# Moving twelve pairs of one batch's feed-forward part from beside the last projections to beside the last causal convolution

## The chip, the cores and the metric

The kernel runs on one core of one Trainium2 chip. The metric is the time of one execution on the device, in microseconds (us). A core has five engines, each with a queue of its own: TensorE (PE in the profile) for matmuls, VectorE (DVE), ScalarE (ACT), GpSimd (POOL) and SyncE (SP), which here only issues transfers. GpSimd issues transfers too. All data are 32-bit floats.

## The reference

Two layers are computed on `x` of shape 4 x 512 x 128 x 64 (4 batches, 512 times, 8192 channels in all). Layer 0, cut to what matters here:

```python
xn = layernorm(x, ln_attn)                    # over the 8192 channels
k, v, r = xn @ Wk, xn @ Wv, sigmoid(xn @ Wr)  # 64 states each
states = scan(s = decay * s + k * v)          # over time
x = x + (r * states) @ Wo
x = x + gelu(conv_freq(layernorm(x, ln_freq)))        # 3 taps over the 128 frequencies
to = conv_time(layernorm(x, ln_time)) + time_b        # causal, 3 taps over time, per channel
x = x + layernorm(to, time_ln)
x = x + gelu(x @ ffn_W1 + b1) @ ffn_W2 + b2           # per group of 64 channels: 64 -> 256 -> 64
```

Layer 1 takes a moving average over time, filters the rest in the frequency domain, and adds both. The change does not touch it.

## The kernel before

**Tiling.** In layer 0 the 8192 channels of a batch are 64 chunks (`NCH`) of 128 partitions with the 512 times along the free dimension; two chunks are a pair (`NPR` = 32), and a transfer moves a pair (512 KB). Between stages a batch lies in DRAM: `x2d` after attention and frequency convolution, `tod` for the outcome of the causal convolution, `x4` after the feed-forward part.

**Stages of a batch.** `project` (J) multiplies the input with the key, value and gate weights; each step is one chunk, with loads of `xp`, of the weights `wx` and of the same input in time order for the statistics, which VectorE takes (L338), and it scales the weights (L355). `scan` (Z) is a long chain over several engines. `attend_and_convolve` (A) adds attention and does the frequency convolution. `convolve_time` (C) normalizes each pair (`normed`, L608 and L611), applies three taps (`tapped`: ScalarE L616, VectorE L620, four half-size operations a pair), squares the outcome, and has TensorE sum both for the next layer norm (`add_up`, L251). `open_feed` (O) spreads the moments of that norm into two rows of 512 times on all partitions (`rows`), and prepares two pairs. `feed_forward` (F) does the rest.

**Inside the feed-forward part.** `residual` loads `kx` (from `x2d`) and `kh` (from `tod`) and normalizes with two full-size VectorE operations (L686, L687). `add_residual` scales on ScalarE (L695) and adds on VectorE (L698). Per chunk, `widen` (L718) makes two products with the first weights into the tiles `m` and `c`, each followed by a GELU on ScalarE (L722) into `mid`; `narrow` (L729) multiplies with the second weights into `pa`, a PSUM tile of which there is one, and VectorE adds bias and residual while it evicts it (L734); `store` (L743) transposes on TensorE, ScalarE copies into `ob`, and GpSimd sends a transfer for every two pairs.

**Order.** TensorE's instructions stand in the order in which the program writes them (`manual_schedule`); a scheduler orders the other engines' queues, except where `keep_in_program_order` pins one. `in_turn` writes two lanes side by side: each line of its table holds two stages (or groups of stages) of different batches, each stage yields weights that add up to its share, and the lane that is behind goes on, with a lead that a list gives for each line. `needed` holds a stage back until its input exists. The lines around the change are:

```python
((1, (O, 0.05), (F, 0.95)), (3, (J, 0.88), (Z, 0.12))),
((2, (C, 1.0)), (3, (A, 1.0))),
((2, (O, 0.05), (F, 0.95)), (3, (C, 0.95), (O, 0.05))),
((3, (F, 1.0)), (3, (nothing, 1.0))),
```

So batch 1's feed-forward part goes beside batch 3's projections and scan, batch 2's beside batch 3's causal convolution, and batch 3's alone. While the feed-forward parts of batches 0 and 1 run, `convolve_ahead` makes the first 14 pairs (`AHEAD`) of the next batch's causal convolution, one step (`normed` or `tapped`) with every second chunk from the fifth on.

**Rows.** The spread rows live in single buffers by name: `rm`, `rm3` and `rm4`. A stage whose rows use a name waits until the last reader of the former rows is done.

Of the kernel before, what the change touches and what calls it, by code (L numbers as in the profile page):

```python
# [16 lines left out]
P = 128  # L17
# [4 lines left out]
NCH = D // P  # L22
SL = 512
NS = D // SL
NPR = NCH // 2
# [54 lines left out]
def layer0(ctx, tc, dram, x, xt, vecs, wkvr, wo, wdec, wconv, fbias, w1, fb1, w2, fb2, x4):  # L80
# [560 lines left out]
    def convolve_time(b):  # L641
        bank = of_a if b == B - 1 else of_p
        made = AHEAD if b in ahead else 0
        moment = carried.pop(b)
        if made:
            rb, mb = ahead.pop(b)
        else:
            rb, mb = yield from rows(bank, *moment, "rm" if b == B - 1 else "rm3")
        st = bank()
        waiting, added = [], 0  # L650
        n = NPR - made
        for k in range(n + 2):
            while waiting and waiting[0][0] == k - 2:
                add_up(st, 0, *waiting.pop(0)[1:], added == 0, added == NPR - 1)
                added += 1
            if k < n:
                if b == B - 1:

                    x2, xr, to, sq = spare("xp", SL), spare("x1", SL), spare("z", SL), two(bk, "sq")
                else:  # L660
                    x2 = bk.tile([P, 2, SL], F32, tag="kx", name="x2", bufs=3)
                    xr, to = two(bk, "kd"), bk.tile([P, 2, SL], F32, tag="k3", name="to", bufs=3)
                    sq = bk.tile([P, 2, SL], F32, tag="sq4", name="sq4", bufs=2)

                normed(b, made + k, x2, xr, rb, mb, made > 0 and k < 4)
                tapped(b, made + k, xr, to)
                nc.scalar.activation(sq, to, AF.Square)
                waiting.append((k, to, sq))
                i = k * made // n
                if i != (k + 1) * made // n:  # L670

                    to = fetch("kh", tod, b, i)
                    sq = bk.tile([P, 2, SL], F32, tag="mid", name="sq5", bufs=4)
                    nc.scalar.activation(sq, to, AF.Square)
                    waiting.append((k, to, sq))
            yield 7.0 * (NPR + 2) / (n + 2)
        mean, sq = yield from finish(st, bank, 4)
        causal[b] = moments(mean, sq, 4)

# [20 lines left out]

    def open_feed(b):
        last = b == B - 1
        scale[b] = yield from rows(of_a if last else of_p, *causal.pop(b), "rm3" if last else "rm4")
        opened[b] = {}
        for i in range(2):
            opened[b][i] = add_residual(b, i, *residual(b, i))
            yield CHAIN

    def feed_forward(b):
        x3s = opened.pop(b)  # L710
        mids, x4s, obs = {}, {}, {}

        def widen(c, m):
# [24 lines left out]
        def store(c):  # L738
# [2 lines left out]
            pt = pool.tile([P, NT, P], F32, tag=tag, name="pt")  # L741
            for t in range(NT):
                nc.tensor.transpose(pt[:, t, :], x4t[:, t * P : (t + 1) * P], ident)  # L743
            s = c // 4
            if c % 4 == 0:
                obs[s] = bk.tile([P, NT, SL], F32, tag="ob", name="ob")
            o = obs[s][:, :, c % 4 * P : (c % 4 + 1) * P]
            if c // 2 % 2:
                for h in range(2):
                    nc.scalar.copy(o[:, :, halves[1 - h]], pt[:, :, halves[h]])  # L750
            else:
                nc.scalar.copy(o, pt)
            if c % 4 == 3:
                nc.gpsimd.dma_start(
                    x4[b][:, s * SL : (s + 1) * SL].rearrange("(t p) d -> p t d", p=P), obs.pop(s)
                )

        early = None
        for c in range(NCH + 2):
            if c < NCH:  # L760
                widen(c, 0)
                widen(c, 1)
            i = c // 2 + 2
            if i < NPR:
                if c % 2:
                    x3s[i] = add_residual(b, i, *coming)
                else:
                    coming = residual(b, i)
            if 0 < c <= NCH:
                narrow(c - 1)  # L770
            if c > 1:
                store(c - 2)
            if b + 2 < B and c > 4 and c % 2:
                early = early or convolve_ahead(b + 1)
                next(early, None)
            yield 4.5

# [6 lines left out]
    def run(b, stages):  # L784
        for stage, share in stages:
            for weight in stage(b):
                yield BLOCKED if weight == BLOCKED else weight * share / whole[stage]

    def in_turn(leads, *pairs):
        at, running = [0.0, 0.0], [None, None]  # L790
# [26 lines left out]
    def nothing(b):  # L817
        yield 1.0

    J, Z, A, C, O, F = project, scan, attend_and_convolve, convolve_time, open_feed, feed_forward  # L820
    begin[A] = 0
    needed = {A: scanned, C: carried, O: causal, F: opened}
    whole = {
        J: 2.0 * NPR, Z: 7 * CHAIN, A: 7.0 * NPR + 3 * CHAIN, C: 7.0 * (NPR + 2) + 3 * CHAIN, O: 4 * CHAIN,
        F: 4.5 * (NCH + 2), nothing: 1.0,
    }
    with tc.manual_schedule(engines={nc.tensor.engine}):
        for _ in project(0):
# [7 lines left out]
            ((1, (C, 1.0)), (2, (A, 1.0))),  # L836
            ((1, (O, 0.05), (F, 0.95)), (3, (J, 0.88), (Z, 0.12))),
            ((2, (C, 1.0)), (3, (A, 1.0))),
            ((2, (O, 0.05), (F, 0.95)), (3, (C, 0.95), (O, 0.05))),
            ((3, (F, 1.0)), (3, (nothing, 1.0))),  # L840
        )

# [298 lines left out]
```

## Time and profile before

| | |
|---|---|
| median of 3 runs | 3780.76 us (3776.11 to 3791.31) |
| the profiled execution | 3802.5 us, its span 3800.7 us |
| mean granted TensorE clock | 0.975 |
| TensorE busy | 3636.3 us (96%) |
| VectorE busy | 2683.6 us (71%) |
| ScalarE busy | 1761.2 us (46%) |
| GpSimd busy | 513.3 us (14%) |
| moved by DMA | 912.80 MB, mean 240 GB/s |

Busy time is what an engine's own instructions cover; matmuls overlap each other, so a busy TensorE is not one at its peak. In the span's order the stretches that matter are: to 1498 us all that lies ahead of batch 1's feed-forward part; from 1498 to 1835 that part beside the projections of batch 3; to 1892 its last chunks beside the scan of batch 3; to about 2130 the attention stage of batch 3 beside the causal convolution of batch 2; to about 2149 the change of stages; to about 2503 batch 2's feed-forward part beside batch 3's causal convolution and what follows it; from there to 2791 batch 3's feed-forward part alone; and then layer 1.

### The profile page before, as it was taken

What the parts mean: (1) busy time and instruction counts of PE and PEld (TensorE: products, weight loads), DVE (VectorE), ACT (ScalarE), POOL (GpSimd) and SP (SyncE); (2) the same over time, 40 slices, a digit from 0 to 9 for tenths busy, and PEclk for the clock granted to TensorE, in tenths of its full rate; (3) what the DMA queues carried; (4) which work ended last, traced back from release to release, by engine and by line L of the source; (5) the groups of instructions that cost most, each with busy time, mean ns of one, the idle gap of its engine ahead of it and who ended that gap; (6) DMA issues with size and microseconds to landing.
All of it is one profiled execution on the core that took longest, in us unless ns stands there. A gap on an engine that the chain in (4) does not pass through costs nothing. (4 is left out here: it accounts for less than half of the span.)

```text
span 3800.7 us, 44873 instructions
## 1 busy us (share of the span) xinstructions
PE 3636.3 (96%) x15945; PEld 1345.5 (35%) x15945; DVE 2683.6 (71%) x3498; ACT 1761.2 (46%) x2491; POOL 513.3 (14%) x782
## 2 busy tenths in 40 slices
PE   9989999999999999999999988999989999999998
PEld 4433322223333223333322322333322843327533
DVE  4445559976777896677789799755567277892677
ACT  0013336645656565566656678867744210142100
POOL 0000012210011221011122221100012000131001
PEclk9999989999999899999999999999999999999999
DMA  9867647786874788787478677545567478993687
GB/s 310 272 203 242 229 146 264 254 288 241 287 280 169 247 285 287 251 278 278 172 258 282 205 249 262 202 155 177 183 222 246 146 236 295 309 294 140 205 296 264
DMA packets 429175, 912.80 MB, mean 240 GB/s; under 512 B 33240, under 2 KB 83608, under 8 KB 424856
## 3 DMA queue, kind: packets, MB, share of 16 engines
q1 hardware_dynamic: 351024, 636.87, 49.7%
q0 software_dynamic: 75776, 271.62, 20.5%
q8 instruction: 127, 2.08, 0.2%
q10 hardware_dynamic: 2152, 1.45, 0.1%
q14 instruction: 96, 0.79, 0.1%
HBM read 641.31 MB, written 268.50 MB: 239 GB/s over the span
## 5 line engine op out<-in xcount | busy, mean ns | idle before, releaser
L729 PE MATMUL pa<-mid,w_sb 128*64 128x512 f32 x2048 | 500.2, 609 | 37.2 <-DVE x4t L734 37.2
L734 DVE SCALAR_TENSOR_TENSOR x4t<-pa,fb_sb,x 128x512 f32<-128x512 f32 x252 | 188.4, 748 | 345.7 <-PE pa L729 345.6
L722 ACT ACTIVATE mid<-m,fb_sb 128x1024 f32<-128x1024 f32 x256 | 285.1, 1114 | 280.5 <-PE m L718 280.2
L718 PE MATMUL m<-x,w_sb 64*128 64x512 f32 x1008 | 290.4, 649 | 0.4 <-ACT mid L722 0.4
L722 ACT ACTIVATE mid<-c,fb_sb 128x1024 f32<-128x1024 f32 x256 | 283.2, 1106 | 1.5 <-PE c L718 1.5
L718 PE MATMUL c<-x,w_sb 64*128 64x512 f32 x1008 | 263.4, 596 | 1.3 <-ACT mid L722 1.3
L729 PEld LDWEIGHTS pa<-mid,w_sb 128*64 128x64 f32 x2048 | 125.0, 136 | 379.9 <-issue 250.8
L406 PE MATMUL a<-xp,wx 128*128 128x512 f32 x512 | 240.7, 596 | 0.5 <-DVE me L268 0.5
L986 ACT COPY two<-a 128x512 f32<-128x512 f32 x64 | 37.5, 586 | 425.0 <-PE a L981 425.0
L1009 PE MATMUL b<-xin,avg_sb 128*128 128x512 f32 x512 | 230.8, 593 | 2.3 <-DVE xin L1015 2.3
L1015 DVE TENSOR_TENSOR xin<-b,pm 128x512 f32<-128x512 f32 x256 | 159.1, 684 | 95.6 <-PE b L1012 80.7
L567 ACT ACTIVATE sq<-x 128x1024 f32<-128x1024 f32 x128 | 135.0, 1054 | 180.5 <-DVE x L564 180.5
L620 DVE SCALAR_TENSOR_TENSOR to<-kd,vec,to 128x510 f32<-128x510 f32 (+1 forms) x272 | 197.8, 746 | 16.0 <-ACT to L616 10.4
L695 ACT ACTIVATE kd<-kd,vec 128x512 f32<-128x512 f32 x256 | 193.3, 809 | 3.1 <-DVE kd L687 3.1
L891 DVE COPY xf<-b 128x256 f32<-128x256 f32 x128 | 54.4, 425 | 185.3 <-PE b L955 173.2
L912 DVE TENSOR_TENSOR uv<-xin 128x1024 f32<-128x1024 f32 x128 | 155.4, 1227 | 39.4 <-DMA xin<-x 18.9
L251 PE MATMUL st<-x,ones 128*32 128x512 f32 x512 | 169.4, 611 | 13.3 <-DVE x L564 13.1
L743 PEld LDWEIGHTS pt<-ident,x4t 128*128 128x128 f32 x1024 | 107.7, 141 | 208.7 <-ACT mid L722 152.5
L528 DVE TENSOR_TENSOR x<-a,xp 128x1024 f32<-128x1024 f32 x128 | 156.2, 1220 | 33.6 <-PE a L526 31.1
L620 DVE SCALAR_TENSOR_TENSOR z<-x,vec,z 128x511 f32<-128x511 f32 x240 | 175.8, 745 | 5.7 <-ACT z L616 2.3
L526 PE MATMUL a<-rst,wo_sb 64*128 64x512 f32 x512 | 153.1, 672 | 27.2 <-DVE x L528 23.2
L743 PE MATMUL pt<-ident,x4t 128*128 128x128 f32 x1024 | 168.8, 288 | 1.5 <-ACT ob L750 1.5
(241 smaller groups left out, 6532.8 us busy)
## 6 DMA issues: line engine op xcount, KB each, us to landing
xp<-in_xt SPq DMA_DIRECT2D x256, 512.0 KB
xin<-x SPq DMA_DIRECT2D x128, 1024.0 KB
kh<-to SPq DMA_DIRECT2D x156, 512.0 KB
x<-x POOLq DMA_DIRECT2D x128, 512.0 KB, 4.4
kx<-x SPq DMA_DIRECT2D x128, 512.0 KB
x<-ob POOLq DMA_DIRECT2D x64, 1024.0 KB, 6.3
out<-xin POOLq DMA_DIRECT2D x64, 1024.0 KB, 7.1
x<-x SPq DMA_DIRECT2D x96, 512.0 KB
```

The source lines that it names most:

```text
L251: nc.tensor.matmul(st[32 * q : 32 * q + 32, :], lhsT=ones, rhs=src[:, j, :], start=first, stop=last,)
L406: nc.tensor.matmul(pa[:, k, :], lhsT=wq[:, j, k * P : (k + 1) * P], rhs=xp[:, j, :], start=first and j == 0, stop=last and j == 1,)
L528: nc.vector.tensor_tensor(x1, at, xp, ALU.add)
L620: tap = nc.vector.scalar_tensor_tensor(to[:, j, k:], xr[:, j, : SL - k], vec[:, w, c], to[:, j, k:], ALU.mult, ALU.add)
L695: tc.keep_in_program_order(nc.scalar.activation(d[:, j, :], d[:, j, :], AF.Identity, bias=vec[:, B4, c], scale=vec[:, G4, c]))
L718: nc.tensor.matmul(pm[:, h, :], lhsT=w1_sb[hs, m * P : (m + 1) * P], rhs=x3[hs, :], start=True, stop=True)
L722: nc.scalar.activation(mid, pm, AF.Gelu_apprx_tanh, bias=fb1_sb[:, m : m + 1])
L729: nc.tensor.matmul(pa[h * H : (h + 1) * H, :], lhsT=w2_sb[:, m, :], rhs=mid[:, h, :], start=(m == 0), stop=(m == 1),)
L734: nc.vector.scalar_tensor_tensor(x4t, pa, fb2_sb, x3s[c // 2][:, c % 2, :], ALU.add, ALU.add)
L743: nc.tensor.transpose(pt[:, t, :], x4t[:, t * P : (t + 1) * P], ident)
L1009: nc.tensor.matmul(po[j], lhsT=avg_sb[:, j, :], rhs=xin[:, j, :], start=True, stop=False)
L1015: nc.vector.tensor_tensor(by_n(xin[:, j, :]), by_n(po[j]), by_c(pm[j % 2][:, j // 2, :]), ALU.add)
```

## The change

Batch 1's feed-forward part stops after 20 of its 32 pairs (`LATE` = 12 are left). The stage that was batch 2's feed-forward part becomes `feed_late` (L), which runs over a list of 44 pairs: the 12 of batch 1, then the 32 of batch 2. The body of `feed_forward` becomes `feed`, which takes such a list. The first two late pairs are prepared by `open_late` at the end of batch 2's causal convolution; the rows of batch 2's norm (`scale_rows`) are made beside the first chunks of `feed_late` and go into `rm3`, and batch 3's go into `rm4`. Batch 1's feed-forward part takes a step of `convolve_ahead` with every chunk rather than every second. `run` scales the weights of the shortened stage. The number of matmuls, of operations on the other engines and of bytes moved stays the same.

```diff
--- before.py
+++ after.py
@@ -674,6 +674,8 @@
                     nc.scalar.activation(sq, to, AF.Square)
                     waiting.append((k, to, sq))
             yield 7.0 * (NPR + 2) / (n + 2)
+        if b == 2:
+            yield from open_late(b)
         mean, sq = yield from finish(st, bank, 4)
         causal[b] = moments(mean, sq, 4)
 
@@ -700,14 +702,36 @@
 
     def open_feed(b):
         last = b == B - 1
-        scale[b] = yield from rows(of_a if last else of_p, *causal.pop(b), "rm3" if last else "rm4")
+        scale[b] = yield from rows(of_a if last else of_p, *causal.pop(b), "rm4")
         opened[b] = {}
         for i in range(2):
             opened[b][i] = add_residual(b, i, *residual(b, i))
             yield CHAIN
 
+
+    LATE = 12
+
     def feed_forward(b):
-        x3s = opened.pop(b)
+        yield from feed(opened.pop(b), [(b, i) for i in range(NPR - LATE if b == 1 else NPR)])
+
+    def feed_late(b):
+
+        late = [(b - 1, i) for i in range(NPR - LATE, NPR)]
+        yield from feed(opened.pop(b), late + [(b, i) for i in range(NPR)], scale_rows(b))
+
+    def scale_rows(b):
+        scale[b] = yield from rows(of_p, *causal.pop(b), "rm3")
+
+    def open_late(b):
+        opened[b] = {}
+        for i in range(2):
+            at = NPR - LATE + i
+            opened[b][i] = add_residual(b - 1, at, *residual(b - 1, at))
+            yield CHAIN
+
+    def feed(x3s, pairs, beside=()):
+
+        beside = iter(beside)
         mids, x4s, obs = {}, {}, {}
 
         def widen(c, m):
@@ -741,37 +765,40 @@
             pt = pool.tile([P, NT, P], F32, tag=tag, name="pt")
             for t in range(NT):
                 nc.tensor.transpose(pt[:, t, :], x4t[:, t * P : (t + 1) * P], ident)
-            s = c // 4
-            if c % 4 == 0:
+            b, i = pairs[c // 2]
+            s, k = i // 2, i % 2 * 2 + c % 2
+            if k == 0:
                 obs[s] = bk.tile([P, NT, SL], F32, tag="ob", name="ob")
-            o = obs[s][:, :, c % 4 * P : (c % 4 + 1) * P]
-            if c // 2 % 2:
+            o = obs[s][:, :, k * P : (k + 1) * P]
+            if i % 2:
                 for h in range(2):
                     nc.scalar.copy(o[:, :, halves[1 - h]], pt[:, :, halves[h]])
             else:
                 nc.scalar.copy(o, pt)
-            if c % 4 == 3:
+            if k == 3:
                 nc.gpsimd.dma_start(
                     x4[b][:, s * SL : (s + 1) * SL].rearrange("(t p) d -> p t d", p=P), obs.pop(s)
                 )
 
         early = None
-        for c in range(NCH + 2):
-            if c < NCH:
+        first, n = pairs[0][0], 2 * len(pairs)
+        for c in range(n + 2):
+            if c < n:
                 widen(c, 0)
                 widen(c, 1)
             i = c // 2 + 2
-            if i < NPR:
+            if i < len(pairs):
                 if c % 2:
-                    x3s[i] = add_residual(b, i, *coming)
+                    x3s[i] = add_residual(*pairs[i], *coming)
                 else:
-                    coming = residual(b, i)
-            if 0 < c <= NCH:
+                    coming = residual(*pairs[i])
+            if 0 < c <= n:
                 narrow(c - 1)
             if c > 1:
                 store(c - 2)
-            if b + 2 < B and c > 4 and c % 2:
-                early = early or convolve_ahead(b + 1)
+            next(beside, None)
+            if first + 2 < B and len(pairs) <= NPR and c > 4 and (c % 2 or first == 1):
+                early = early or convolve_ahead(first + 1)
                 next(early, None)
             yield 4.5
 
@@ -784,7 +811,8 @@
     def run(b, stages):
         for stage, share in stages:
             for weight in stage(b):
-                yield BLOCKED if weight == BLOCKED else weight * share / whole[stage]
+                part = 1 - LATE / NPR if stage is feed_forward and b == 1 else 1.0
+                yield BLOCKED if weight == BLOCKED else weight * share / whole[stage] / part
 
     def in_turn(leads, *pairs):
         at, running = [0.0, 0.0], [None, None]
@@ -818,11 +846,12 @@
         yield 1.0
 
     J, Z, A, C, O, F = project, scan, attend_and_convolve, convolve_time, open_feed, feed_forward
+    L = feed_late
     begin[A] = 0
     needed = {A: scanned, C: carried, O: causal, F: opened}
     whole = {
         J: 2.0 * NPR, Z: 7 * CHAIN, A: 7.0 * NPR + 3 * CHAIN, C: 7.0 * (NPR + 2) + 3 * CHAIN, O: 4 * CHAIN,
-        F: 4.5 * (NCH + 2), nothing: 1.0,
+        F: 4.5 * (NCH + 2), L: 4.5 * (NCH + 2 * LATE + 2), nothing: 1.0,
     }
     with tc.manual_schedule(engines={nc.tensor.engine}):
         for _ in project(0):
@@ -836,7 +865,7 @@
             ((1, (C, 1.0)), (2, (A, 1.0))),
             ((1, (O, 0.05), (F, 0.95)), (3, (J, 0.88), (Z, 0.12))),
             ((2, (C, 1.0)), (3, (A, 1.0))),
-            ((2, (O, 0.05), (F, 0.95)), (3, (C, 0.95), (O, 0.05))),
+            ((2, (L, 1.0)), (3, (C, 0.95), (O, 0.05))),
             ((3, (F, 1.0)), (3, (nothing, 1.0))),
         )
 
```

## The prediction

> **What bounds the kernel now.** I read the granted clock and span first (one core, clock 0.975 of full, span 3800.7 us inside an execution of 3802.5 us), then the forty slices, then the busy time of stretches whose borders I took from TensorE's order of time, then the waits inside the two stretches that the change touches.
>
> ```profile
> PE   9989999999999999999999988999989999999998
> ...
> DVE  4445559976777896677789799755567277892677
> ...
> DMA  9867647786874788787478677545567478993687
> ```
>
> TensorE is busy nearly everywhere, so only its gaps and its slow-clock spells can be won. A slice is 95 us; the dull place is near slices 22 to 25, where VectorE reads 9. The stretches, with columns length, PE, PE weight loads, VectorE, ScalarE, GpSimd, clock, DMA share and GB/s:
>
> ```profile
> 1498.00:1835.00 337.00, 336.31 (x1331) 124.47 (x1332) 244.20 (x327) 204.01 (x272) 29.48 (x35) 1.00 0.78 271
> 1835.00:1892.00 57.00, 52.18 (x240) 22.41 (x236) 39.52 (x57) 38.97 (x55) 10.35 (x13) 0.94 0.36 126
> 1892.00:2130.00 238.00, 227.35 (x1246) 60.54 (x1250) 199.55 (x204) 135.68 (x185) 46.31 (x68) 0.95 0.75 256
> 2130.00:2149.00 19.00, 14.18 (x80) 7.55 (x74) 13.04 (x15) 9.40 (x13) 3.69 (x4) 0.84 0.58 193
> 2149.00:2434.00 285.00, 250.85 (x1214) 83.79 (x1212) 278.54 (x315) 238.03 (x314) 58.22 (x74) 0.98 0.71 244
> 2434.00:2503.00 69.00, 64.69 (x306) 24.66 (x306) 38.52 (x41) 49.87 (x67) 5.09 (x7) 0.95 0.49 170
> ```
>
> The first row is batch 1's feed-forward beside batch 3's projections: TensorE is the bound (0.7 us idle in 337). The second is the chain of the last scan. The fifth is batch 2's feed-forward beside the last causal convolution: VectorE is the bound (278.5 of 285), TensorE stands 34 us. Its wait, in the list of waits of that stretch (us in total, times, longest), is for VectorE's eviction of the only `pa` bank:
>
> ```profile
> PE pa L729 <- DVE x4t L734: 32.9, 26, 3.9
> ```
>
> and in the groups of TensorE and of VectorE there:
>
> ```profile
> L729 PE MATMUL pa<-mid,w_sb 128*64 128x512 f32 x392 | 97.3, 618 | 32.9 <-DVE x4t L734 32.9
> ```
>
> ```profile
> L620 DVE SCALAR_TENSOR_TENSOR z<-x,vec,z 128x510 f32<-128x510 f32 x64 | 47.4, 746 | 0.8
> ...
> L611 DVE TENSOR_TENSOR x<-x,rm 128x1024 f32<-128x1024 f32 x32 | 39.0, 1221 | 0.7 <-ACT rm L285 0.3
> ```
>
> Where VectorE lets go, the order of time gives the price of a chunk (128 channels) on TensorE: the second starts 5.37 us after the first, with one `add_up` between them, the third 4.37 us later. So a chunk costs 4.37 us, an `add_up` 1.0 us.
>
> ```profile
> 2424.00 1.13 PE L718 MATMUL m<-x,w_sb 64*128 64x512 f32 x4
> ...
> 2429.37 1.13 PE L718 MATMUL m<-x,w_sb 64*128 64x512 f32 x4
> ...
> 2433.74 1.13 PE L718 MATMUL m<-x,w_sb 64*128 64x512 f32 x4
> ```
>
> **What the Trainium skill says.** "PSUM — Partial Sum Buffer", section Engine vs sequencer instructions: the queues of ScalarE, VectorE and GpSimd are strict FIFO, matmuls start and end in program order. The trace agrees: the eviction at L734 stands behind taps already queued, and the matmul behind it waits up to 3.9 us. "DMA: Bandwidth & Descriptors", Specifications, puts the HBM limit of a core at about 358 GB/s; the first stretch here moves 271 at a share of 0.78, which extrapolates to 347. The same page, Issuing engines are not separate DMA queues: SP's and GpSimd's transfers share the 16 engines, so reads and writes are summed below. "TensorE: Matmul & The Clock Gate", Part 1, ties the clock to recent activity; the trace shows 0.84 to 0.95 in the stretches with gaps and 1.00 in the dense one.
>
> **The change, part by part.** Nothing is computed more or less: 12 pairs, 24 chunks, move from the first stretch and the scan chain to the fifth. The order of instructions of both programs gives the counts.
>
> *Projections stretch.* Before, 55 chunks and 54 projection steps lie between its borders; after, 35 chunks and the same 54 steps. A step is 1.81 us and a chunk among them 4.28 (together 6.09, the repeat in the order of time at 1795 to 1832); two row spreads are 2.6. Before: 235.4 + 97.7 + 2.6 = 336, measured 337. After: 149.8 + 97.7 + 2.6 = 250, so -87 if TensorE stays the bound. VectorE: the order has 87 full operations (1.22 us), 85 half ones (0.745), 64 statistics (0.68), 58 weight scalings (0.31) = 231 us; the same sum for before is 272 against 244 busy, so 208 of 250, 83%. DMA: 271 GB/s x 337 us = 91 MB; 20 chunks less are 15.7 MB less (0.75 MiB each: two reads and a write), two pairs more of the convolution ahead are 2.1 MB more; 77.7 MB in 250 us is 311 GB/s, share 0.90. Where every chunk carries a step of that convolution (some 30 chunks), 0.79 + 0.52 + 1.83 projection steps x 0.655 = 2.5 MB per 7.6 us, 331 GB/s, share 0.95. The nearest stage is the first projection, where the DMA sets the pace, with TensorE at 97% of 80 us:
>
> ```profile
> 20.00:100.00 80.00, 77.64 (x206) 33.99 (x205) 36.86 (x76) 0.00 (x0) 1.72 (x17) 1.00 0.92 306
> ```
>
> So I charge +6 us (bounds 0, and +37 if the stretch keeps today's 271 GB/s: 77.7 MB are then 287 us rather than 250). What goes late is SP's queue, in order: a `kx` load blocks while its buffer is held, with `xp` and `wx` of the projections behind it:
>
> ```profile
> SPq L601 <- DVE x L698: 123.2, 24, 6.4
> ...
> SPq L294 <- PE a L406: 40.8, 12, 4.1
> ```
>
> Today those waits are for buffers, not for data, which is slack. Sum: -81.
>
> *Scan chain.* 57 us now, with 9 chunks as cover (38.5). After, 5 chunks (21.4), and the first row spread comes right behind the last projection, with no chunk before it: its wait for GpSimd's `rs`, 2.4 us now, grows by one chunk at most, 4.3; the shorter gaps before L475 and L493 show about 1 us each (L475 to L493 took 5 us, a chunk covers 4.4). 18.5 + 21.4 + 6 = 46: -11.
>
> *Last attention stretch.* Two residual pairs (six full VectorE operations, 7.3 us, four ScalarE ones, four loads on SP) open batch 1's late pairs at its end, where VectorE has 1.5 to 2.5 us free in each step. Hidden there; 7 if that cover is gone. +1.
>
> *The combined stream.* Now: from the last convolution of batch 3 (2134.6) to the first chunk of batch 3's feed-forward (2513.6), 379 us: 14.5 to the first VectorE operation of the causal convolution, 285 for it, 79.5 to the end. After: the convolution's rows come behind some four chunks, so the start takes 0.95 + 2 x 2.15 + 1.94 + 2.1 + 2 + 8.7 + 1.05 + 3.4 (GpSimd's `rs`, as now) + 2.2 = 27. Then the convolution: its 32 pairs now lie over 64 chunks rather than 48 or 49. VectorE has 160 full and 192 half operations, 338 us nominal; before, 138 and 177, nominal 300, took 285, so 0.95 x 338 = 321. TensorE there: 64 x 4.37 + 32 = 312, ScalarE about 91% (238 busy now, plus 15 chunks at 3.6 us, which are two GELUs of 1.11, a scaling of 0.81 and a copy of 0.6; of 321). VectorE and TensorE are nearly level, so I add 3 for waits upon each other (bounds 0 and 30: 1 us a pair). Such levels exist: at 1300 to 1450 TensorE has 148.5 of 150 with VectorE at 136.9. Then 21 chunks follow rather than 16: 79.5 + 5 x 4.37 = 101. Total 27 + 321 + 3 + 101 = 452: +73. Against the 105 us of matmuls that arrive, some 30 us are absorbed in TensorE's present idle time.
>
> The changed row buffers (`rm3`, `rm4`) cost nothing: their last readers end before the new rows are written.
>
> *Sum:* -81 - 11 + 1 + 73 = -18 us on 3802.5, that is -0.47%. The median of the three runs is 3780.76 (the profiled execution is 22 us above it); the same share gives **3763**.
>
> **The rivals.** *The projections stretch becomes the DMA's* (the other side). For: 311 to 331 GB/s is above any stretch of this kind now, and SP's loads stand in one queue. Against: 20 us pieces reach 356, and buffers run ahead. It decides against the change below 77.7 MB / 293 us = 265 GB/s; at 255 it takes 305, 49 more than forecast: 3811. *TensorE and VectorE wait for each other in the combined stream*, 1.25 us a pair more: 40 more, 3803. For: 97% and 100% in strict queues, with ScalarE at 91%. Against: the order of VectorE's work repeats evenly every two chunks, evictions 6.7 and 3.0 us apart, and that fits 9.74 us of TensorE work. *Nothing moves in sum*: chain, start and DMA eat all that is absorbed: 3781. *A better outcome*: with the gaps the slow clock goes too (the fifth stretch now shows 251 us busy for 49 chunks and 28 `add_up`s, which are 242 us at full clock) and the DMA costs nothing: 19 more, 3744.
>
> **How the numbers follow.** Forecast 0.45 (own range 3750 to 3776), better 0.20, nothing 0.12, DMA 0.13, mutual waits 0.10. Range 3735 to 3812, which leaves out part of the two slow cases and a little of the best. Half a per cent (3761.9 and 3799.7) is about what a measurement tells. Faster: 0.20 from the better case, less 0.01, and 0.27 of the forecast's 0.45: 0.46. Slower: 0.23 from the two slow cases and 0.02 of "nothing": 0.25. Same: the rest, 0.29.
>
> **What would show it.** In the profile after: the projections stretch near 256 us with TensorE above 97% and 300 GB/s or more; if it is near 285, the DMA rival holds, and idle time will stand before L406 with a DMA as releaser. The gap before the first spread after the projections near 6 us. In the combined stream 320 to 325 us from the first to the last tap, with TensorE's wait for the `x4t` eviction below 15 us (33 now); if it stays at 30 or more, the mutual waits hold. The last feed-forward (4.37 us a chunk) and layer 1 unchanged. I am wrong if the projections stretch or the tap stretch is off by more than 20 us, or if the attention stretch between them, left almost as it is, grows.

## The result, and the profile after

The changed kernel takes 3815.52 us (median of 4 runs, 3812.84 to 3819.56) against 3784.26 us (4 runs, 3776.11 to 3791.31) for the kernel before on the same chip: a ratio of 1.0084, 95% interval 1.0059 to 1.0109. It is slower by 31 us, where 3763 was forecast, 18 less than before; the range given, 3735 to 3812, leaves it out by 3.5 us. Its profiled execution took 3812.84 us (span 3811.1, clock 0.976).

The stretches of the changed kernel, in the windows view (length, PE, PE weight loads, VectorE, ScalarE, GpSimd, clock, DMA share, GB/s): the projections, the scan chain, the attention stretch, and the combined stream in three parts, up to the first VectorE operation of the causal convolution, up to its last tap, and up to the first chunk of batch 3's feed-forward part.

```profile
1466.60:1734.40 267.80, 266.69 (x988) 104.66 (x988) 211.81 (x304) 141.25 (x190) 30.83 (x38) 1.00 0.90 310
1734.40:1780.70 46.30, 37.60 (x174) 17.58 (x174) 22.13 (x40) 24.86 (x34) 6.21 (x8) 0.89 0.19 64
1780.70:2023.90 243.20, 230.28 (x1263) 60.81 (x1263) 212.53 (x212) 141.31 (x191) 46.01 (x67) 0.96 0.80 269
2023.90:2059.10 35.20, 25.87 (x121) 12.62 (x123) 11.76 (x19) 16.85 (x20) 4.25 (x5) 0.84 0.23 76
2059.10:2433.30 374.20, 331.92 (x1540) 112.43 (x1536) 322.75 (x353) 291.12 (x388) 57.45 (x79) 0.96 0.65 219
2433.30:2534.00 100.70, 93.58 (x450) 35.47 (x446) 51.75 (x55) 69.19 (x93) 5.87 (x9) 0.98 0.48 162
```

Between the same instructions in both traces (first row spread after the former stage, last projection, first attention matmul, last attention convolution, first chunk of batch 3's feed-forward part):

| stretch | before, us | after, us | difference | forecast |
|---|---|---|---|---|
| projections | 355.1 | 267.7 | -87.4 | -81 |
| scan chain | 60.3 | 46.3 | -14.0 | -11 |
| attention | 242.5 | 243.2 | +0.7 | +1 |
| combined stream | 379.0 | 510.1 | +131.1 | +73 |
| the rest | | | -20 | 0 |

The rest is layer 0 before batch 1's feed-forward part (-10) and batch 3's with layer 1 (-10), which the change does not touch: the profiled execution before lies 18 us above the median of its runs, the one after 3 us below. The whole of the miss is in the last stage but one: +131 rather than +73, and there in the 374 us of the taps (324 forecast; 8 us more are in the start). No engine is full in them: TensorE 332, VectorE 323, ScalarE 291 of 374. The groups of that stretch show what stood (busy us, mean ns of one, then the idle time before and what ended it):

```profile
L753 PE MATMUL pa<-mid,w_sb 128*64 128x512 f32 x520 | 131.2, 626 | 40.8 <-DVE x4t L758 40.8
L620 DVE SCALAR_TENSOR_TENSOR z<-x,vec,z 128x510 f32<-128x510 f32 (+1 forms) x128 | 94.2, 748 | 34.8 <-ACT z L616 22.0 <-issue 10.4
L611 DVE TENSOR_TENSOR x<-x,rm 128x1024 f32<-128x1024 f32 x32 | 39.1, 1223 | 0.9
```

TensorE's wait for the eviction of `pa` (L734 before, L758 here) has grown from 32.9 to 40.8 us. VectorE stood 2.9 us at its taps in that stretch of the kernel before (the row of 0.8 in the prediction is one of the two forms of this operation, which are 128 here as there):

```profile
L620 DVE SCALAR_TENSOR_TENSOR z<-x,vec,z 128x510 f32<-128x510 f32 (+1 forms) x128 | 92.5, 746 | 2.9 <-issue 1.8
```

Now it stands 34.8 us there: for 22.0 of them the view names ScalarE's first product (L616), for 10.4 it names no releaser ("issue"). Both engines wait, each for work that depends on the other.

### The profile page after: what moved, and what is told of

It reads as the page before. It is cut to its first block, busy times and chain, and to the rows that moved or that the text cites. A ratio compares the mean times of both kernels' runs of the same rounds, so it can differ in the third digit from the quotient of the medians.

```text
span 3811.1 us, 44860 instructions
## 1 busy us (share of the span) xinstructions
PE 3631.6 (95%) x15945; PEld 1348.8 (35%) x15945; DVE 2689.7 (71%) x3498; ACT 1761.2 (46%) x2491; POOL 506.3 (13%) x782
## 5 line engine op out<-in xcount | busy, mean ns | idle before, releaser
L758 DVE SCALAR_TENSOR_TENSOR x4t<-pa,fb_sb,x 128x512 f32<-128x512 f32 x252 | 188.4, 748 | 336.6 <-PE pa L753 336.2
L406 PE MATMUL a<-xp,wx 128*128 128x512 f32 x512 | 237.9, 597 | 0.5 <-DVE me L268 0.5
L620 DVE SCALAR_TENSOR_TENSOR to<-kd,vec,to 128x510 f32<-128x510 f32 (+1 forms) x272 | 197.7, 745 | 13.3 <-ACT to L616 9.6
L251 PE MATMUL st<-x,ones 128*32 128x512 f32 x512 | 168.0, 611 | 11.7 <-DVE x L564 11.7
L528 DVE TENSOR_TENSOR x<-a,xp 128x1024 f32<-128x1024 f32 x128 | 156.2, 1220 | 31.9 <-PE a L526 29.7
```

Of the source, the lines that this page charges most:

```text
L251: nc.tensor.matmul(st[32 * q : 32 * q + 32, :], lhsT=ones, rhs=src[:, j, :], start=first, stop=last,)
L406: nc.tensor.matmul(pa[:, k, :], lhsT=wq[:, j, k * P : (k + 1) * P], rhs=xp[:, j, :], start=first and j == 0, stop=last and j == 1,)
L528: nc.vector.tensor_tensor(x1, at, xp, ALU.add)
L620: tap = nc.vector.scalar_tensor_tensor(to[:, j, k:], xr[:, j, : SL - k], vec[:, w, c], to[:, j, k:], ALU.mult, ALU.add)
L758: nc.vector.scalar_tensor_tensor(x4t, pa, fb2_sb, x3s[c // 2][:, c % 2, :], ALU.add, ALU.add)
```

## Where in the stretch

`add_up` (L251), four pairs of matmuls that sum a pair's output and its squares, stands in TensorE's order behind every second chunk. In the changed kernel the 32 sums stand behind the second chunk of a pair five times, then 15 times behind the first, then 12 times behind the second again; the two lanes slip by a chunk twice. I call the places behind the second chunk even and those behind the first odd. In time, two even sums are 10.0 us apart (the first few up to 13.7), two odd ones 12.0 to 13.5 us. Here is one odd period, 12.0 us from sum to sum, engine by engine (start, length, operation; in brackets the idle time before it and what ended it). TensorE:

```profile
2239.75 0.62 PE L251 MATMUL a<-z,ones 128*32 128x512 f32 x1
...
2240.75 1.13 PE L742 MATMUL m<-x,w_sb 64*128 64x512 f32 x4
2241.71 1.02 PE L742 MATMUL c<-x,w_sb 64*128 64x512 f32 x4
2242.66 1.94 PE L753 MATMUL pa<-mid,w_sb 128*64 128x512 f32 x8
...
2249.28 1.94 PE L753 MATMUL pa<-mid,w_sb 128*64 128x512 f32 x8 [2.17 <-DVE x4t L758]
2251.14 0.66 PE L767 MATMUL pt<-ident,x4t 128*128 128x128 f32 x4
2251.73 0.62 PE L251 MATMUL a<-z,ones 128*32 128x512 f32 x1
```

ScalarE:

```profile
2240.87 0.81 ACT L616 ACTIVATE z<-x,tb_all,vec 128x512 f32<-128x512 f32 x1 [0.42 <-PE a L251]
```

VectorE:

```profile
2241.77 3.13 DVE L620 SCALAR_TENSOR_TENSOR z<-x,vec,z 128x511 f32<-128x511 f32 x4 [1.48 <-issue]
2244.94 1.23 DVE L608 TENSOR_TENSOR x<-xp,rm 128x1024 f32<-128x1024 f32 x1
2246.20 1.22 DVE L611 TENSOR_TENSOR x<-x,rm 128x1024 f32<-128x1024 f32 x1
2247.34 1.22 DVE L700 TENSOR_TENSOR x<-kd,kx 128x1024 f32<-128x1024 f32 x1
2248.47 0.75 DVE L758 SCALAR_TENSOR_TENSOR x4t<-pa,fb_sb,x 128x512 f32<-128x512 f32 x1
```

Read from start to start, this is a closed ring: each link waits for the one before it, for its result or in its engine's queue, and after the last comes the sum of the next turn. The sum of pair 11 (counted from 0) takes 1.12 us until the first product of pair 15 starts, which waits for it because the output tile has four buffers and takes the one that the sum frees; 0.90 until the taps start (0.09 us after that product's end, though the view writes "issue"); 3.17 for four taps; 2.40 for the next pair's two scalings; 1.13 for a residual add; 0.81 for the eviction; then TensorE's `pa` matmuls, which had waited 2.17 us for it, 1.86; the transposes 0.59; then the next sum. 1.12 + 0.90 + 3.17 + 2.40 + 1.13 + 0.81 + 1.86 + 0.59 = 11.98 us, the measured period. There is no stop anywhere in this chain, yet each engine has only about 10 us to do in a turn: TensorE 2 x 4.37 + 1.0 = 9.7, VectorE 10.0 (its turn in the run e10 below, where it works without a gap).

In an even place VectorE's order is another: the eviction follows on the last tap at once, not three operations later. So it stands in the experiment e1 below, again in order of time:

```profile
2240.55 0.74 DVE L758 SCALAR_TENSOR_TENSOR x4t<-pa,fb_sb,x 128x512 f32<-128x512 f32 x1
2241.21 1.22 DVE L700 TENSOR_TENSOR x<-kd,kx 128x1024 f32<-128x1024 f32 x1
...
2245.39 2.19 DVE L620 SCALAR_TENSOR_TENSOR z<-x,vec,z 128x510 f32<-128x510 f32 x3
2247.50 0.74 DVE L758 SCALAR_TENSOR_TENSOR x4t<-pa,fb_sb,x 128x512 f32<-128x512 f32 x1
```

There too the first product waits for a sum (8.9 us in 23 waits), but VectorE has other work meanwhile and its taps wait 0.8 us in all. That the closed ring, and not the amount of work, is the cause was the theory for the experiments. The rivals: TensorE and VectorE are simply both full (with the one `pa` buffer as the wait to remove), or VectorE's order in the odd part is dear by itself.

## The experiments

The times, each beside runs of the kernel before on the same chip (ratio with its 95% interval):

| run | edit | us | ratio to before |
|---|---|---|---|
| after | | 3815.5 | 1.0084 (1.0059 to 1.0109) |
| e1_even | all sums even | 3772.1 | 0.9973 (0.9962 to 0.9983) |
| e2_odd | all sums odd | 3857.1 | 1.0191 (1.0173 to 1.0209) |
| e3_lag1 | sums one step behind their pair | 3811.0 | 1.0076 (1.0056 to 1.0095) |
| e4_pa2 | second `pa` | 3808.2 | 1.0068 (1.0046 to 1.0089) |
| e5_even_pa2 | e1 and second `pa` | 3770.1 | 0.9965 (0.9948 to 0.9982) |
| e6_before_pa2 | before with second `pa` | 3799.7 | 1.0046 (1.0034 to 1.0057) |
| e7_buffers | six output buffers | 3823.0 | 1.0109 (1.0093 to 1.0125) |
| e8_even_buffers | e1 and six output buffers | 3778.8 | 0.9987 (0.9973 to 1.0001) |
| e9_fixed_sums | sums read fixed tiles | 3813.0 | 1.0080 (1.0060 to 1.0100) |
| e10_held | first products held back | 3759.8 | 0.9942 (0.9922 to 0.9961) |
| e11_even_held | e1 and held back | 3762.5 | 0.9952 (0.9935 to 0.9969) |
| e12_before_held | before, held back | 3775.0 | 0.9979 (0.9966 to 0.9992) |

### The place of the sums

```diff
-            (0.12, 0.12, 0.08, 0.04, 0.08, 0.02, -0.05, 0.08, 0.0),
+            (0.12, 0.12, 0.08, 0.04, 0.08, 0.02, -0.05, 0.115, 0.0),
```

In e1 one of the leads of the two lanes is changed, nothing else; the 32 sums then all stand in even places. In e2, the second edit below, two leads are changed, and all 32 stand in odd places.

> One number differs from the changed kernel: the lead of the combined stage at its end is 0.115 rather than 0.08, so that all 32 sums of the causal convolution stand behind every second chunk, always behind the second chunk of a pair (in the changed kernel 15 of them stand behind the first). Theory (a ring): behind the first chunk, the release of a z buffer by the sum, ScalarE's first tap, VectorE's four taps, the next pair's normalization, the eviction queued behind them and the matmul that waits for it form a closed ring of 12.0 us a pair (13.4 at the slow clock); behind the second chunk 10.0. Then the tap stretch takes 32 x 10.02 = about 321 to 326 us rather than 374, and the kernel about 3764 us, 0.995 of before. Rival (three engines near full, the place makes no difference): tap stretch about 374 and time 3815, as the changed kernel.

```diff
-            (0.12, 0.12, 0.08, 0.04, 0.08, 0.02, -0.05, 0.08, 0.0),
+            (0.12, 0.12, 0.08, 0.04, 0.08, 0.02, -0.07, 0.10, 0.0),
```

> Leads -0.07 and 0.10 for the combined stage: all sums of the causal convolution stand behind the first chunk of a pair. The ring theory: about 26 to 28 pairs at 12.0 to 13.4 us rather than 15, so 25 to 45 us more in the tap stretch than in the changed kernel (400 to 420 us), time 3840 to 3860, 1.015 to 1.020 of before. Rival (the place makes no difference): 3815.

Measured: 3772.1 and 3857.1 us, 85 us apart with the same instructions on every engine. In e1 the sums come every 10.0 us and the taps take 325 us, which is what the prediction had (324); in e2 they come every 13.5 us or so while the taps last. The stretch of even sums, in the windows of e1:

```profile
2140.00:2370.00 230.00, 225.60 (x1106) 76.82 (x1104) 223.74 (x250) 209.06 (x277) 41.25 (x57) 1.00 0.76 252
```

and, for comparison, the odd part of the changed kernel:

```profile
2160.00:2346.00 186.00, 155.56 (x703) 51.53 (x704) 148.38 (x160) 131.19 (x175) 26.07 (x36) 0.93 0.61 206
```

TensorE goes from 84% to 98%, VectorE from 80% to 97%. So the place of the sums sets the time: the fifth sum and the twenty-first lie 211.1 us apart in the changed kernel and 160.1 in e1. Two chunks more (8.7 us) are made between them in the changed kernel, which leaves some 42 us of loss, near the 40 by which the two streams differ (510.1 and 470.0). What this pair of runs does not tell is why an odd place is dear.

### The single buffer of `pa`

TensorE's largest wait is for the one `pa` buffer. The idle half of the PSUM tile that holds the sums serves as a second one, for odd chunks.

```diff
-        st = bank()
+        both = two(ps_a, "a") if b == B - 1 else None
+        st, second[0] = (both[:, 0, :], both[:, 1, :]) if both is not None else (bank(), None)
...
-            pa = ps_p.tile([P, SL], F32, tag="p", name="pa")
+            pa = second[0] if c % 2 and second[0] is not None else ps_p.tile([P, SL], F32, tag="p", name="pa")
```

> The changed kernel with a second pa bank: while the last causal convolution runs, every second chunk's pa goes into the idle half of the two-bank tile that holds its sums. 15 sums stand behind the first chunk of a pair as in the changed kernel, and VectorE's order there is the same. The ring theory: the matmul into pa (1.87 us) leaves the ring, since it no longer waits for the eviction just before it; the ring is 11.98 - 1.87 = 10.1 us, so these pairs take 10.1 to 10.4 us, the tap stretch about 325 to 335 us rather than 374, time 3766 to 3775. Rival (VectorE's order of work there is bad by itself, or the release of the z buffer alone sets the pace): 12 us or more a pair, time 3810 or more.

> All sums behind the second chunk of a pair (as in e1_even), and the second pa bank. If the 10.01 us a pair of e1_even are TensorE's own 2 x 4.37 + 1.0 = 9.74 and a wait of 0.2 us for each eviction, a pair falls to 9.75 to 9.9 us and the kernel to 3762 to 3769. If they are VectorE's work, nothing changes: 3772.

> The kernel before with the second pa bank. If VectorE is the bound of its tap stretch, as the prediction read it (278 of 285 us busy), the bank changes nothing beyond 0.2%: 3775 to 3785. If TensorE's 33 us of waits for the eviction are a ring there too, up to 30 us fall away: 3750 to 3760.

In e4 the odd part still takes 12.7 to 13.5 us a pair, and the kernel 3808.2 us, not the 3766 to 3775 that I had expected of the ring. Its TensorE and VectorE in order of time:

```profile
2262.42 0.94 PE L251 MATMUL a<-z,ones 128*32 128x512 f32 x1 [2.12 <-DVE x4t L760]
```

```profile
2261.53 0.74 DVE L760 SCALAR_TENSOR_TENSOR x4t<-a,fb_sb,x 128x512 f32<-128x512 f32 x1
2265.25 3.13 DVE L620 SCALAR_TENSOR_TENSOR z<-x,vec,z 128x511 f32<-128x511 f32 x4 [2.97 <-issue]
```

The matmul no longer waits, but the sum does: it writes one half of a tile whose other half VectorE is evicting, and it starts when that eviction ends. The wait changed its place and a ring stayed: now VectorE's run from the taps to its second eviction, then the sum, then the first product, which waits 45.8 us for sums over the odd part (10.3 in the changed kernel). So e4 did not try a second buffer that is free of the sums; what that would bring is not shown. The same edit costs the kernel before 16 us (e6), which neither way of the expectation had: there too the sums now wait for evictions (31.9 us), and the first product's waits for a sum grow from 7.9 to 38.5 us. Where the sums are even it brings nothing (e5, 10.0 us a pair as in e1).

### Three tries at opening the ring

```diff
-            while waiting and waiting[0][0] == k - 2:
+            while waiting and waiting[0][0] == k - (1 if b == B - 1 else 2):
```

> The changed kernel, but in the last causal convolution each pair's sum is written one step (about two chunks) earlier, one step behind its pair rather than two; 15 sums still stand behind the first chunk of a pair and VectorE's order of work there is the same as in the changed kernel. The ring theory: the z buffer comes free one step earlier, the ring is open, ScalarE's first tap no longer waits for TensorE, those pairs take 10.0 to 10.5 us, the tap stretch about 325 to 335, time 3764 to 3778, 0.995 to 0.998 of before. Rival (the order of the evictions among the taps is what costs, or full engines, not the release of the buffer): 12 us or more a pair and about 3815.

```diff
-                    x2, xr, to, sq = spare("xp", SL), spare("x1", SL), spare("z", SL), two(bk, "sq")
+                    to, sq = two(bk, "x2") if k % 3 == 2 else spare("z", SL), spare("wx", 4 * S + SL)[:, :, 0:SL] if k % 2 else two(bk, "sq")
+                    x2, xr = spare("xp", SL), spare("x1", SL)
```

> The changed kernel with six buffers in place of four for the last causal convolution's output, and four in place of two for its squares (idle tiles of the sequences' earlier stages are used); the sums stay where the changed kernel has them, 15 of them behind the first chunk of a pair. In the written order the convolution now stands two pairs further ahead of the feed-forward part than in the changed kernel, as many as there are more buffers, so a pair's first product again waits for the sum that stands just before it. Theory (ring through sums, first product, taps, VectorE's order, eviction and projection): the ring is as closed as before, the 15 pairs take 12.0 to 13.5 us each, time 3800 to 3820. Rival (four buffers are too few in themselves): these pairs take 10 to 10.5 us, tap stretch about 325 to 335, time 3766 to 3780.

> The same six and four buffers, with all 32 sums behind the second chunk of a pair as in the first experiment (3772). Theory (there VectorE's own 9.6 to 10 us of work a pair is the limit, not a wait for a buffer): 10.0 us a pair again, time 3766 to 3778. Rival (the ring still costs there too): under 9.8 us a pair, time 3755 to 3763.

```diff
-                waiting.append((k, to, sq))
+                waiting.append((k, pair_of(mb), pair_of(rb)) if b == B - 1 else (k, to, sq))
```

> The changed kernel, where the sums of batch 3's causal convolution read two fixed tiles (its scale and offset rows) in place of the pair's output and its squares: as many matmuls of the same size at the same places in TensorE's order, 15 of them behind the first chunk of a pair, but no first product and no square waits for a sum any more, and the statistics of batch 3's last normalisation are those of other numbers (the computation is changed in this). The convolution's tiles then come free with the store, and VectorE's order becomes less regular, with the taps further ahead. Theory (ring): from the last attention convolution to batch 3's last feed-forward part 460 to 480 us (510 in the changed kernel, 470 in the first experiment), time 3765 to 3785. Rival (the place of the sums in TensorE's order is dear by itself, or the odd VectorE order that goes with it): 500 to 515 us, time 3800 to 3820.

e3 (3811.0, where I had expected 3764 to 3778) and e7 (3823.0) left the odd part at 12 us and more. Neither opened the ring, so neither speaks against it. The scheduler that orders the other engines moves the convolution as far ahead as the buffers allow: in e3, where a sum comes one step earlier, the first product stands one pair further ahead; in e7, with two buffers more, two pairs. In the written order of all three kernels, the first product waits for the sum right before it. In e3 and in e7 the first product starts 1.1 to 1.8 us after that sum, as in the changed kernel. For e3 I read this only after the run; for e7 it was in the expectation, and it came out so. e8 shows the other side: with even sums two more buffers bring no gain (3778.8 against 3772.1).

e9 went against my expectation: 3813.0, not 3765 to 3785, though no first product waits for a sum. The odd sums come 9.7 to 16.8 us apart, and the combined stream takes 514 us, which is what the rival had (500 to 515). Its windows, ahead of the last taps and behind them, say where it went:

```profile
2150.00:2345.00 195.00, 165.55 (x757) 53.50 (x756) 174.89 (x200) 155.44 (x207) 52.11 (x49) 0.96 0.66 229
2345.00:2440.00 95.00, 95.00 (x472) 32.92 (x472) 51.77 (x50) 65.20 (x89) 3.76 (x5) 1.00 0.48 166
```

With nothing to hold it the convolution ran far ahead of the chunks. VectorE has the taps of more pairs in the first window (175 us busy of 195, 200 operations where the changed kernel has 160 in 186 us), TensorE starves there, and in the second VectorE is half idle. The run changed VectorE's order as much as it removed the wait, so it doesn't separate the two; on its figure alone the rival (a dear order) would have stood.

### The first products held back

What separates them is a kernel with the sums at the same odd places and VectorE's order all but the same, in which the first product needs a sum that is long done. One more constraint does it: each first product of the last causal convolution stays behind the ScalarE instruction that the program issues before it.

```diff
-    def tapped(b, i, xr, to, pinned=False):
+    def tapped(b, i, xr, to, pinned=False, held=False):
...
-            nc.scalar.activation(
+            first = nc.scalar.activation(
                 to[:, j, :], xr[:, j, :], AF.Identity, bias=tb_all[:, c], scale=vec[:, W2, c]
-            )
+            ) ; j == 0 and held and tc.keep_in_program_order(first)
...
-                tapped(b, made + k, xr, to)
+                tapped(b, made + k, xr, to, held=b == B - 1)
```

> The changed kernel with one constraint more: each first product of the last causal convolution is kept behind the ScalarE instruction that the program issues before it, so the convolution no longer runs two pairs ahead of its sums. All work is done; the sums stay where the changed kernel has them, behind the first chunk of a pair in the middle part; VectorE's order there is the same but for one exchange (four taps, next pair's two scalings, eviction, residual, the two residual scalings, eviction). With four buffers the first product of a pair then needs a sum that was made two pairs earlier, and waits for none. Theory (ring through the sum and the buffer): 10.0 to 10.6 us a pair in that part, time 3765 to 3785. Rival (the place of the sums, or VectorE's order that goes with it, is dear by itself): 12 us and more a pair, time 3800 to 3820. A third way: the constraint closes another chain (output copy, first product, taps, eviction), which by the durations of the changed kernel adds to about 10.3 us, and if it is longer the time lies between.

> The same constraint with all 32 sums behind the second chunk of a pair. Theory: 10.0 us a pair as without the constraint, time 3765 to 3780. Rival (the constraint costs by itself): over 10.3 us a pair, time over 3785.

> The kernel before with the same constraint (first products of the last causal convolution kept behind the ScalarE instruction issued before them): what the constraint brings without the change. VectorE's work there, from the rows of the kernel before, is about 9.5 us a pair of the convolution (two scalings, four taps, and 1.6 chunks of residual and eviction), 304 us for 32 pairs, where the stretch took about 321. If the waits of that stretch came from the same ring: 5 to 17 us less, time 3765 to 3778, so that the change is then worth 5 to 18 us (3760 with it). If they did not: no difference, 3778 to 3785, and the change with the constraint is worth about 20 us, nearly what the sum of the prediction had.

e10 takes 3759.8 us, a little less than the 3765 to 3785 expected: the 15 odd pairs come every 10.01 us. The first product of pair 15 now stands behind the sum of pair 12, and the sum of pair 11, which it needs, started 11.4 us earlier (1.12 in the changed kernel). Its windows there:

```profile
2143.00:2298.00 155.00, 152.17 (x746) 52.04 (x744) 152.00 (x169) 140.44 (x185) 25.87 (x38) 1.00 0.78 259
```

In the list of waits of the odd part (us in total, times, longest) the changed kernel has

```profile
PE pa L753 <- DVE x4t L758: 30.4, 14, 2.2
...
DVE z L620 <- ACT z L616: 22.0, 8, 2.9
...
ACT z L616 <- PE a L251: 10.3, 15, 1.1
```

The first is TensorE's at the `pa` matmuls, the second VectorE's at the taps, the third the first product's for a sum, 15 times. In the odd part of e10 the third is gone from the list, and of the others there is left:

```profile
PE pa L753 <- DVE x4t L758: 2.8, 14, 0.2
...
DVE z L620 <- ACT z L616: 1.2, 1, 1.2
```

VectorE in e10, in order of time over one odd pair:

```profile
2219.01 0.74 DVE L758 SCALAR_TENSOR_TENSOR x4t<-pa,fb_sb,x 128x512 f32<-128x512 f32 x1
2219.67 2.72 DVE L620 SCALAR_TENSOR_TENSOR z<-x,vec,z 128x511 f32<-128x511 f32 x4
2222.31 1.22 DVE L608 TENSOR_TENSOR x<-xp,rm 128x1024 f32<-128x1024 f32 x1
2223.56 1.23 DVE L611 TENSOR_TENSOR x<-x,rm 128x1024 f32<-128x1024 f32 x1
2224.70 0.74 DVE L758 SCALAR_TENSOR_TENSOR x4t<-pa,fb_sb,x 128x512 f32<-128x512 f32 x1
2225.37 1.22 DVE L700 TENSOR_TENSOR x<-kd,kx 128x1024 f32<-128x1024 f32 x1
2226.61 1.23 DVE L688 TENSOR_TENSOR kd<-kh,rm 128x1024 f32<-128x1024 f32 x1
2227.88 1.22 DVE L689 TENSOR_TENSOR kd<-kd,rm 128x1024 f32<-128x1024 f32 x1
2229.02 0.74 DVE L758 SCALAR_TENSOR_TENSOR x4t<-pa,fb_sb,x 128x512 f32<-128x512 f32 x1
```

The taps follow the last eviction at once. The order differs from the changed kernel's by one exchange, eviction before residual, which takes 1.1 us out of the ring; that alone would leave 10.9 us. So the sums' place is not dear by itself: the ring was the cause, and the measured 10.01 us is VectorE's own sum of work, from one eviction (2219.01) to the same one of the next turn (2229.02) without a gap. That the exchange by itself does not do it is an argument from the ring's sum; no run has the exchange without the hold. The third way of the expectation (a chain through the output copy, about 10.3) did not show.

e11 (3762.5) confirms that with the ring open the place of the sums no longer matters: 3759.8 with 15 odd and 3762.5 with all even, intervals overlapping. The constraint is worth something outside the odd part too. It takes 0.21%, some 8 us, off the kernel before (e12), where the first product waits for a sum as well (7.9 us in 19 waits; whether these waits are what it removes there is not shown), and 0.21% off e1 (e11 against e1; these two intervals overlap). In the changed kernel it takes off 1.42% (1.0084 to 0.9942), some 54 us; less those 8, some 46 are left for the odd part, near the 42 counted above. The best version here is e10, faster than before by 0.39 to 0.78%; of that the moved pairs are worth some 14 us (0.9942 over 0.9979 is 0.9963; an estimate, good to about 9 us by the two intervals).

## Why the prediction was wrong, point by point

**The projections, -81.** Right in mechanism, and better than said: -87.4. The 6 us charged for the DMA are not there. In three windows of 50 us TensorE is busy throughout while the transfers run at shares of 0.94 to 0.96:

```profile
1550.00:1600.00 50.00, 50.00 (x186) 18.93 (x185) 43.59 (x63) 28.36 (x38) 8.63 (x10) 1.00 0.94 329
1600.00:1650.00 50.00, 50.00 (x187) 18.94 (x186) 44.19 (x61) 28.30 (x39) 7.31 (x8) 1.00 0.94 322
1650.00:1700.00 50.00, 50.00 (x187) 18.92 (x185) 43.79 (x63) 28.53 (x39) 8.13 (x10) 1.00 0.96 329
```

The estimate of 331 GB/s at 0.95 for these steps held. "DMA: Bandwidth & Descriptors", Specifications, puts a core's limit at about 358 GB/s; 329 is 92% of it, and costs nothing here. Nor did that figure bind in this case: from 1557 to 1577 us this core moved 382 GB/s, with TensorE busy for 20.00 of the 20 us. The rival of the DMA is refuted by its own sign: 0.3 us of idle time before L406, none of it for a transfer, and a stretch of 268 us, where the rival's 305 would be 323 in these borders (they begin 18 us earlier than the prediction's 337 us).

**The scan chain, -11.** -14.0; the wait for GpSimd's `rs` right behind the last projection is 6.3 us, as said.

**The attention stretch, +1.** +0.7.

**The combined stream, +73.** Wrong by 58, in two of its three terms. The start took 35.2 us, not 27: TensorE stood 5.2 us, not 3.4, at the second row spread, and at a clock of 0.84 many of the small products among them took about 2.0 us, not 1.1. The tail, 101, came out at 100.7. The tap stretch took 374 rather than 321 + 3: this is the step that failed, 50 us of the 58. It took VectorE's work at the rate of the former stretch (0.95 x 338), put 3 us on it for mutual waits, and took the pattern of one pair for that of all 32: "the order of VectorE's work repeats evenly every two chunks, evictions 6.7 and 3.0 us apart, and that fits 9.74 us of TensorE work". That is the even order, and 17 of the 32 pairs have it; I had not looked where the sums stand in TensorE's order over the whole stretch. Nor does a sum of an engine's work hold when the work of three engines closes a ring: there the period is the length of the ring, 11.98 us at a clock of 1.00, though no engine has more than about 10 us to do. "PSUM — Partial Sum Buffer", section Engine vs sequencer instructions, was cited for strict queues; the trace shows what I should have concluded from it, that an eviction behind taps which wait holds the sum on which the taps wait.

**The rivals.** "TensorE and VectorE wait for each other" was the true one in kind, at 1.25 us a pair, 40 us in all and a chance of 0.10. Its sign came too: TensorE's wait for the eviction stayed above 30 us (40.8). The waits are instead 2 to 3.5 us in the 15 odd pairs and next to none in most of the others, and what links them, the sum and ScalarE's first product, is not in the rival; that its total is near is luck. Of the better case only the clock came true, and only once the ring was open: 1.00 in the tap stretch of e10 and 0.99 in that of e1, against 0.96 in the changed kernel. Its time, 3744, is the median of no run. The prediction's reading that the clock is 0.84 to 0.95 in the stretches with gaps passes over its own fifth row, with 34 us of gaps at 0.98.

**The sum, -18.** With the ring open, the stream of e10 is 461.0 us (from 2019.4, the last attention convolution, to 2480.4), +82 against the kernel before. With the measured terms of the other stretches, -87.4 - 14.0 + 0.7 + 82 = -19. That this is so near to -18 is in part luck: the stream is still 9 us longer than forecast (+73), and the projections and the scan chain are together 9 us better. The timed runs give -22 us for e10 against before, and -14 against before with the same constraint. So the two great terms, what the projections gain and what the stream can absorb, had the right size to within 9 us each, and the ring, which the sum left out, turned the sign.

## What to carry to other kernels

Where several in-order queues pass work round through tiles with few buffers, list the chain from one instruction to the same instruction of the next turn and add it up, as was done for the 11.98 us; compare that with each engine's own work, and do it for every phase of the interleaving, not for the first one that is seen. A wait taken out of such a ring can come back at another place (e4), and more buffers can be used up by a scheduler that runs ahead (e7); letting the early work run less far ahead opened it here (e10). When two lanes are interleaved by shares, a shift by one chunk can be worth more than the change under study: here 85 us between all even and all odd.

## What the runs showed of the hardware that I had not expected

The odd period is longer where the granted clock is lower. At a clock of 1.00 (2230 to 2260 us in the changed kernel) it is 12.0 us; from 2160 to 2230, at 0.88, it is 13.3 to 13.5. In e2 the `pa` matmuls behind the wait take 3.1 us rather than 1.94:

```profile
2259.73 1.94 PE L753 MATMUL pa<-mid,w_sb 128*64 128x512 f32 x8
2266.34 3.13 PE L753 MATMUL pa<-mid,w_sb 128*64 128x512 f32 x8 [2.17 <-DVE x4t L758]
```

These are eight products of the same form; the second group stands in the ring, and 11.98 + 1.19 = 13.2 is most of the way to 13.5. The gap before it does not by itself set its length: in the changed kernel groups behind the same gap take from 1.94 us (at 2249.28 above) to 2.77:

```profile
2169.46 2.77 PE L753 MATMUL pa<-mid,w_sb 128*64 128x512 f32 x8 [2.17 <-DVE x4t L758]
```

The mean clock is 0.93 over the odd part of the changed kernel, 1.00 over the even part of e1 and 1.00 over the odd part of e10, which has no such gaps. Whether the gaps bring the clock down, or only go with it, no run here separates.
